# Layer 2's experts by tiles of slots, with weights addressed by registers, and first loads in another order

## The chip, the cores and the metric

The kernel runs on one core of one Trainium2 chip. The metric is the device time of one execution in microseconds (us), as a median of runs. All arithmetic is in float32.

## What is computed

Four decoder-like layers act one after the other on 4 sequences of 512 tokens with 256 features. Each normalises its input and adds an attention part and a feed-forward part to it:

```python
xn = _layernorm(x); x = x + mamba2(xn) + glu(xn)                  # layer 0
xn = _layernorm(x); x = x + latent_attention(xn) + product_key_experts(xn)   # layer 1
xn = _layernorm(x); x = x + head_mix(xn) + _L2_ffn_ref(xn, ...)   # layer 2
xn = _layernorm(x); x = x + full_attention(xn) + top_p_experts(xn)  # layer 3

def _L2_ffn_ref(x, gate_w, wg, wu, wd, sg, su, sd):   # E, K, I = 8, 2, 128
    scores = jax.nn.softmax(jnp.einsum('th,eh->te', xf, gate_w), axis=-1)
    topk_w, topk_i = jax.lax.top_k(scores, K)
    topk_w = topk_w / jnp.sum(topk_w, axis=-1, keepdims=True)
    cw = jnp.zeros_like(scores).at[jnp.arange(T)[:, None], topk_i].add(topk_w)
    g = jnp.einsum('th,ehi->eti', xf, wg)
    u = jnp.einsum('th,ehi->eti', xf, wu)
    eo = jnp.einsum('eti,eih->eth', jax.nn.silu(g) * u, wd)
    y = jnp.einsum('te,eth->th', cw, eo)
    shared = jax.nn.silu(xf @ sg) * (xf @ su) @ sd
    return y + shared
```

So in layer 2 every token has weights for two of eight experts of 128 hidden features each, and a shared expert of 256 hidden features besides. The reference computes all eight for every token; six of the eight weights are zero.

## The kernel before, in words

The residual `x` (16 tiles of 128 tokens by 256 features) and its normalised, transposed copy `xnT` (features on partitions) stay on the chip all the time. `layernorm(c, b)` does one sequence `b`: statistics and scaling on VectorE (lines 94 to 105), then, some pieces later, transposes on TensorE (line 114) that ScalarE copies into `xnT` (line 117). With an argument `tokens` it also writes the rows to a tensor in HBM (line 108), from which layer 1 reads.

Each layer is a set of Python generators that issue a piece of work and yield a number, its assumed cost. `weave` (line 205) always goes on with the generator whose share of its total is smallest, which fixes the program's order; a start of 0.95 lets a stream begin when the others stand at 95 per cent. The framework under it sets the waits and the buffers and may place an engine's instructions in another order than the program's where it estimates that one is ready earlier; `keep_in_program_order` holds one back from that. `c.parts(n, then)` says how many streams must report a sequence with `part_done` before `then` (a `layernorm`, or the store at the end) is issued for it.

Matrix products go through two helpers, `project` (line 125: weights stationary, tokens moving, 512 columns) and `project_tokens` (line 133). `glu_pieces` (line 156) computes a gated unit for one sequence after the other: for each 128 hidden features two products into PSUM, Silu on ScalarE (line 186), a product on VectorE (line 187), and then, for each tile of 128 tokens, the product down (line 194), which `add_scaled` adds to `x` (line 142, or line 144 with a factor per token).

Layer 2 (`layer2`, line 1174) has two streams. `ahead` does `head_mix` and `top2_weights` per sequence: the router's softmax and the rank of each expert by comparisons (`router`, line 1136) give `cw`, a weight per token and expert that is zero but for two. `expert_pieces` (line 1202) takes all eight experts as two units of 512 hidden features, four experts each; with `split=4` each expert's output is scaled by its column of `cw` on its way into `x`. Every token thus goes through all eight. The shared expert follows for each sequence.

Layer 1 has the latent attention (a stream of 457), the product-key experts (232), which gather rows of a table with indirect DMAs from GpSimd (line 917, 8 per tile of tokens), and a gated unit (193). Layer 3 has the full attention and, from 0.95 of it on, eight experts of 512 hidden features. At the start `program` loads `x` in four pieces on SyncE's queue and two tensors of constants on ScalarE's, then layer 0's first weights follow on SyncE's.

## Time and profile before

| | |
|---|---|
| median of 3 runs | 3283.12 us (3281.36 to 3287.85) |
| profiled execution | 3294.33 us, span of its instructions 3292.6 us |
| granted TensorE clock, mean | 0.989 |
| TensorE matmul (PE) busy | 3187.1 us, 97% |
| VectorE (DVE) busy | 1888.8 us, 57% |
| ScalarE (ACT) busy | 1259.1 us, 38% |
| GpSimd (POOL) busy | 565.3 us, 17% |
| DMA | 165.15 MB, mean 50 GB/s |

In the profile PE is TensorE's matmul, PEld its weight load, DVE is VectorE, ACT ScalarE, POOL GpSimd, SP SyncE. A line of a group of instructions gives line of the code, engine, operation, output and inputs, shapes and count, then after the bar the busy time in us and the mean of one in ns, and after the next bar the engine's idle time just before them and what ended it. A line of the order of time gives start and length in us (several alike are put together), and in brackets the idle time before it and its releaser. A "q" behind an engine's name means its sequencer. Matmuls are pipelined and their ends are modelled, so a busy PE is not PE at its peak. A duration comes from this one execution.

### The profile page before, as it was taken

The numbers are of one execution on the slowest core, as the hardware profiler recorded it, in microseconds if no ns is written. First come the engines' busy times: TensorE is split into PE (matmuls) and PEld (weight loads), VectorE is DVE, ScalarE is ACT, GpSimd is POOL, SyncE is SP. The second block draws the span as 40 slices with busy tenths as digits, with TensorE's granted clock in tenths as the row PEclk, the third lists the DMA queues.
The fourth block names the chain that finished last, engine by engine and source line by source line (L and its number), as shares of the span: only waits on it lengthen the run. The fifth ranks groups of instructions, "written<-read, shape, count | busy, mean of one in ns | idle before, by whom it ended". The sixth has DMA issues, their size and how long they took to land.

```text
span 3292.6 us, 35469 instructions
## 1 busy us (share of the span) xinstructions
PE 3187.1 (97%) x12524; PEld 1916.8 (58%) x12524; DVE 1888.8 (57%) x4720; ACT 1259.1 (38%) x2876; POOL 565.3 (17%) x445
## 2 busy tenths in 40 slices
PE   8999999998899999999999999999999999999999
PEld 4555656565555555555665556656656665555555
DVE  4777878887676776767665555455455522222222
ACT  4434444442455655657422333333333321111111
POOL 0455556546200122221010000000000000000000
PEclk9999999999999999999999999999999999999999
DMA  3232323323201343433000100000000010000000
GB/s 125 75 109 94 120 84 109 103 93 99 80 15 34 68 127 95 110 76 96 15 0 20 39 1 26 1 20 7 0 20 0 1 38 18 19 18 19 6 0 26
DMA packets 75650, 165.15 MB, mean 50 GB/s; under 512 B 12368, under 2 KB 46288, under 8 KB 70608
## 3 DMA queue, kind: packets, MB, share of 16 engines
q1 hardware_dynamic: 64368, 127.20, 12.0%
q0 software_dynamic: 10240, 33.56, 4.2%
q8 instruction: 99, 1.62, 0.2%
q10 hardware_dynamic: 864, 2.12, 0.2%
q14 instruction: 79, 0.65, 0.1%
HBM read 149.08 MB, written 4.85 MB: 47 GB/s over the span
## 4 chain that ended last, share of the span: by engine, by line
PE 76%; DVE 11%; DMA 4%; POOL 3%; ACT 3%; issue 2%; SPq 0%; another core or an unknown queue 0%; ACTq 0%; DVEq 0%; POOLq 0%
PE mm L125 31%; PE acc L194 10%; PE mm L577 8%; PE mm L133 4%; PE acc L1034 4%; PE acc L593 3%; DMA G<-own 3%; DVE cy L259 2%; DVE G L400 2%; PE tr L1026 2%; PE tr L756 2%; PE acc L800 2%; PE acc L813 2%; PE tr L486 1%; POOL y L449 1%
## 5 line engine op out<-in xcount | busy, mean ns | idle before, releaser
L125 PE MATMUL mm<-xnT,wu 128*128 128x512 f32 x2384 | 1074.6, 596 | 8.9 <-DVE cy L259 4.9
L125 PEld LDWEIGHTS mm<-xnT,wu 128*128 128x128 f32 x2384 | 450.4, 191 | 506.6 <-issue 472.0
L584 ACT ACTIVATE pr<-pr,nm 128x128 f32<-128x128 f32 (+3 forms) x512 | 286.0, 559 | 313.7 <-DVE nm L580 296.2
L186 ACT ACTIVATE sg<-mm 128x512 f32<-128x512 f32 x200 | 119.0, 595 | 681.6 <-PE mm L125 681.2
L187 DVE TENSOR_TENSOR hT<-sg,mm 128x512 f32<-128x512 f32 x200 | 137.0, 685 | 422.7 <-PE mm L125 408.1
L194 PE MATMUL acc<-wu,hT 128*128 128x256 f32 x1600 | 373.5, 381 | 0.0
L194 PEld LDWEIGHTS acc<-wu,hT 128*128 128x128 f32 x1600 | 299.6, 190 | 89.0 <-issue 34.8
L580 DVE CUSTOM_DVE_ANT_0 pr<-mm,late 128x128 f32<-128x128 f32 (+3 forms) x512 | 245.4, 483 | 99.8 <-PE mm L577 91.6
L125 PE MATMUL mm<-xnT,w_in 128*128 128x512 f32 x512 | 232.7, 599 | 6.1 <-DVE cy L259 4.5
L144 DVE SCALAR_TENSOR_TENSOR x<-acc,cw,x 128x256 f32<-128x256 f32 x256 | 123.4, 483 | 181.1 <-PE acc L194 175.8
L917 POOL DMA_INDIRECT e<-in_p_experts,ids x128 | 127.6, 997 | 506.3 <-DVE x L144 474.6
L400 DVE TENSOR_TENSOR_SCAN G<-G,eye 128x1024 f32<-128x1024 f32 x64 | 159.5, 2492 | 57.2 <-DMA G<-own 57.0
L577 PE MATMUL mm<-kf,qf 128*128 128x128 f32 (+3 forms) x512 | 176.4, 444 | 9.0 <-DVE qf L735 6.0
L577 PE MATMUL mm<-k,q 128*128 128x128 f32 (+3 forms) x512 | 178.5, 438 | 1.1 <-issue 0.9
L426 POOL TENSOR_TENSOR G<-G,CB 128x1024 f32<-128x1024 f32 x64 | 151.1, 2361 | 158.7 <-ACT CB L352 81.0
L259 DVE SCALAR_TENSOR_TENSOR cy<-mm,ws,cy 128x509 f32<-128x509 f32 (+2 forms) x216 | 158.6, 741 | 29.3 <-ACT cy L255 26.0
L125 PEld LDWEIGHTS mm<-xnT,w_in 128*128 128x128 f32 x512 | 97.4, 192 | 111.1 <-issue 98.4
L412 ACT ACTIVATE xD<-xc,ws 128x128 f32<-128x128 f32 x256 | 84.3, 391 | 200.3 <-POOL y L449 194.4
L142 DVE TENSOR_TENSOR x<-acc,x 128x256 f32<-128x256 f32 x176 | 74.0, 422 | 139.8 <-PE acc L593 102.5
L1034 PE MATMUL acc<-PT,V 128*128 128x512 f32 (+3 forms) x512 | 150.2, 436 | 0.0
L999 DVE TENSOR_SCALAR q<-mm,bias 128x512 f32<-128x512 f32 x64 | 48.1, 751 | 169.9 <-PE mm L125 169.9
L486 PE MATMUL tr<-wo,y 128*128 128x256 f32 x512 | 130.1, 398 | 9.4 <-DVE x L142 3.8
(246 smaller groups left out, 4649.7 us busy)
## 6 DMA issues: line engine op xcount, KB each, us to landing
G<-own SPq DMA_DIRECT2D x64, 512.0 KB
w_in<-in_m_units SPq DMA_DIRECT2D x16, 1024.0 KB
eb<-since SPq DMA_DIRECT2D x96, 128.0 KB
wu<-in_o_units SPq DMA_DIRECT2D x8, 1536.0 KB
wo<-in_m_units SPq DMA_DIRECT2D x16, 512.0 KB
psw<-pes SPq DMA_DIRECT2D x128, 64.0 KB
wu<-in_g_units SPq DMA_DIRECT2D x4, 1536.0 KB
wu<-in_f_units SPq DMA_DIRECT2D x4, 1536.0 KB
```

The lines of the kernel that those rows point to most:

```text
L125: c.nc.tensor.matmul(out, lhsT=w[:, d, cols], rhs=c.xnT[:, d, tokens], start=(d == 0), stop=(d == 1))
L133: c.nc.tensor.matmul(out, lhsT=c.xnT[:, d, tokens], rhs=w[:, d, cols], start=(d == 0), stop=(d == 1))
L187: nc.vector.tensor_mul(h, sg, pu)
L194: nc.tensor.matmul(po, lhsT=hT[k][:, t * P : (t + 1) * P], rhs=wd[:, k, :], start=(i == 0), stop=(i == per - 1),)
L259: nc.vector.scalar_tensor_tensor(y[:, j:], src[:, : SEQ - j], conv[:, k, 3 - j : 4 - j], y[:, j:], ALU.mult, ALU.add,)
L400: nc.vector.tensor_tensor_scan(flat, flat, eye.rearrange("p h t -> p (h t)"), 0.0, ALU.mult, ALU.add)
L426: nc.gpsimd.tensor_mul(G, G, seqs[b][2][:, t, :][:, None, :].to_broadcast([P, HG, P]))
L486: nc.tensor.matmul(po, lhsT=y[:, k, :], rhs=groups[i][1][:, k, :], start=(k == 0), stop=(k == 3))
L577: nc.tensor.matmul(sc, lhsT=q[:, i * P : n], rhs=k[:, :n], start=True, stop=True)
L580: nc.vector.tensor_tensor_reduce(out=pr, in0=sc, in1=late[:, SEQ - n :], scale=1.0, scalar=-NEG, op0=ALU.add, op1=ALU.min, accum_out=nm,)
L584: nc.scalar.activation(pr, pr, AF.Exp, bias=nm, scale=-1.0, accum_out=total)
L1034: nc.tensor.matmul(z[:, j * P :], lhsT=head["V"][:, j, h, :], rhs=head["PT"][:, j, j * P :], start=(j == 0), stop=(j == TPB - 1),)
```

## The change

Layer 2's tokens are treated in two halves of 1024 (`Half`). `dispatch` ranks the experts as before and then, for each token and each of its two experts, computes a slot: tokens of one expert get consecutive slots, and each expert's slots are filled up to a multiple of 128, at most 23 tiles of slots per half. It yields `ids` (which token stands in a slot), `slot` (where a token's two results will be), `weight`, and `expert` (where the weights of each tile's expert begin). `experts` goes through the 23 tiles in pairs: an indirect DMA gathers the normalised rows of a tile's tokens, TensorE turns them, and one expert's matrices, taken out of a tile with all weights at a column held in a register of TensorE, are applied; the results are written to HBM by slots. `combine` gathers each token's two rows and adds them with their weights to `x`.

The order changes with it. The first half's `dispatch` is a fourth stream of layer 1 from 0.915 on, after the buffers of two other streams were closed; layer 1's `layernorm` writes its rows to HBM for the gathers. `Layer2.run` issues the second half's `dispatch`, then weaves the first half's experts with `head_mix` and the shared expert, then the second half's experts with the first half's `combine`. The second half's `combine` is a stream of layer 3. The buffers of several stages change sides in SBUF. Layer 3 adds its output bias per sequence in the third group of heads instead of at its start. At the kernel's start `first_loads` issues all first loads on SyncE's queue: `x` in five pieces, between them the identity alone, the first unit's gate and up weights in two parts, and the rest of the constants and the down weights last; `layernorm` of the input moves into `layer0`.

```diff
@@ layernorm
-            r = b * SEQ + t * P
-            nc.sync.dma_start(tokens[r : r + P, :], xn)
+            nc.sync.dma_start(tokens[t * P : (t + 1) * P, :], xn)
@@ layer0
+def first_loads(c, a, x_in, con, ws, unit):
+    nc = c.nc
+    load = nc.sync.dma_start
+    def tokens(lo, hi):
+        load(
+            c.x[:, lo:hi, :], x_in[lo * P : hi * P, :].rearrange("(t p) d -> p t d", p=P)
+        )
+    def chunks(k):
+        part = lambda v: v[:, :2048].rearrange("p (m j) -> p m j", j=512)[:, :, k * P : (k + 2) * P]
+        load(part(unit), part(a["g0_units"][0]))
+    tokens(0, 2)
+    tokens(2, 4)
+    load(con[:, :P], a["constants"][:, :P])
+    chunks(0)
+    tokens(4, 8)
+    load(ws, a["m_small"])
+    tokens(8, 12)
+    tokens(12, 16)
+    chunks(2)
+    load(con[:, P:], a["constants"][:, P:])
+    load(unit[:, 2048:], a["g0_units"][0][:, 2048:])
+def layer0(c, a, x_in, con):
...
+        unit = c.tile(c.weights, [P, 3072], "wu")
+        ws = c.tile(open_pool("m_ws", 1), [P, 762], "ws")
+        first_loads(c, a, x_in, con, ws, unit)
+        for b in range(NB):
+            layernorm(c, b)
+            c.step(True)
...
+        def glu_units():
+            same = dict(bufs=5, out_tag="tr")
+            yield from glu_pieces(c, glu, [unit], loaded=True, last=False, **same)
+            yield from glu_pieces(c, glu, [a["g0_units"][1]], first=1, **same)
+        c.parts(2, lambda b: layernorm(c, b, c.xn[b * SEQ : (b + 1) * SEQ, :]))
...
@@ layer1
+def layer1(c, a, xn, following):
+    with ExitStack() as stack, ExitStack() as right:
+        def pool_of(name, bufs, stack=stack, **kw):
+            return stack.enter_context(c.tc.tile_pool(name=name, bufs=bufs, **kw))
+        p_keep, p_t, glu = (pool_of(name, 1, right, side="right") for name in ("p_keep", "p_t", "g1"))
+        dram = pool_of("p_dram", 1, space=bass.MemoryType.DRAM)
+        keep = pool_of("l_keep", 1)
         prep = c.tc.tile_pool(name="l_pre", bufs=2)
         latent = latent_pieces(c, a, keep, prep, lambda: pool_of("l_h", 2))
+        def route():
+            right.close()
+            yield from following.route()
         weave(
             c,
             (latent, 457.0, 0.0),
             (product_key_pieces(c, a, p_keep, p_t, dram, xn), 232.0, 0.0),
             (glu_pieces(c, glu, [a["g1_units"][u] for u in range(2)], tanh=True, bufs=5), 193.0, 0.0),
+            (route(), 150.0, 0.915),
         )
...
@@ full_attention
-        for t in range(NTILE):
-            nc.gpsimd.tensor_add(c.x[:, t, :], c.x[:, t, :], bias[:, 48:])
...
+                    if g == 2:
+                        nc.gpsimd.tensor_add(c.x[:, tt, :], c.x[:, tt, :], bias[:, 48:])
@@ layer 2
-def top2_weights(c, pool, wr, cw, b):
...
-def layer2(c, a):
...
-def expert_pieces(c, pool, a, by_token):
...
+E8, HT, NS = 8, NTILE // 2, 23
+EW = 6 * P
+class Half:
+    def __init__(self, c, k, pool, keep, dram, hf, xn):
+        self.c, self.k, self.pool, self.hf, self.xn = c, k, pool, hf, xn
+        self.out = c.tile(dram, [NS * P, DM], "slots_out")
+        new = lambda shape, tag, dtype=F32: c.tile(keep, shape, tag, dtype, bufs=2)
+        self.ids = new([P, NS], "ids", U32)
+        self.slot = new([P, 2 * HT], "slot", U32)
+        self.weight = new([P, 2, HT], "weight")
+        self.expert = new([P, NS], "expert", I32)
+    def dispatch(self):
+        c, k, pool, nc = self.c, self.k, self.pool, self.c.nc
+        tile = lambda shape, tag, **kw: c.tile(pool, shape, tag, **kw)
+        p, rank = tile([P, HT, E8], "p_half"), tile([P, HT, E8], "rank")
+        for i in range(2):
+            tiles = slice(i * TPB, (i + 1) * TPB)
+            before = router(c, pool, k["router"], 2 * self.hf + i, p[:, tiles, :])[2]
+            nc.vector.tensor_reduce(rank[:, tiles, :], before, AX.X, ALU.add)
+            yield 1.0
+        both = [P, 2, HT, E8]
+        sel = tile(both, "sel")
+        for r in range(2):
+            nc.vector.tensor_scalar(sel[:, r], rank, float(r), None, ALU.is_equal)
+        chosen = tile([P, HT, E8], "chosen")
+        nc.vector.tensor_scalar(chosen, rank, 2.0, None, ALU.is_lt)
...
+        pc = c.ps()
+        n = HT * E8
+        nc.tensor.matmul(pc[:, :n], lhsT=c.le, rhs=flat(chosen), start=True, stop=False)
+        nc.tensor.matmul(pc[:, :n], lhsT=c.ones, rhs=flat(cum[:, :HT, :]), start=False, stop=True)
+        nc.tensor.matmul(
+            pc[:, n : n + E8], lhsT=c.ones, rhs=cum[:, HT, :], start=True, stop=True
+        )
+        yield 1.0
...
+        nc.vector.tensor_mul(pick, sel, place[:, None, :, :].to_broadcast(both))
+        nc.vector.tensor_reduce(
+            slot, pick.rearrange("p r t e -> p (r t) e"), AX.X, ALU.add
+        )
+        nc.vector.tensor_copy(self.slot, slot)
+        yield 1.0
...
+        pid = c.ps()[:, :NS]
+        for i in range(2 * HT):
+            at = tile([P, P], "at", bufs=3)
+            t = i % HT
+            nc.vector.tensor_scalar(
+                at, k["iota"], part[:, i : i + 1], k["token"][:, t : t + 1],
+                ALU.is_equal, ALU.mult,
+            )
+            nc.tensor.matmul(
+                pid, lhsT=at, rhs=hit[:, i, :], start=(i == 0), stop=(i == 2 * HT - 1)
+            )
+            if i % 4 == 3:
+                yield 1.0
+        nc.vector.tensor_copy(self.ids, pid)
...
+        nc.vector.tensor_copy(self.expert[:1], where[:1])
+        yield 1.0
...
+    def experts(self, weights, xpool, pool, opool):
+        c, nc = self.c, self.c.nc
+        pairs = [[t for t in (2 * j, 2 * j + 1) if t < NS] for j in range((NS + 1) // 2)]
+        xs, xsT, hs, hT = {}, {}, {}, {}
+        def gather(j):
+            xs[j] = c.tile(xpool, [P, 2, DM], "xs", bufs=3)
+            for i, t in enumerate(pairs[j]):
+                nc.gpsimd.indirect_dma_start(
+                    out=xs[j][:, i, :], out_offset=None, in_=self.xn,
+                    in_offset=bass.IndirectOffsetOnAxis(ap=self.ids[:, t : t + 1], axis=0),
+                )
+        def turn(j):
+            pt = c.ps("tr")
+            n = len(pairs[j])
+            for i in range(n):
+                for d in range(2):
+                    nc.tensor.transpose(
+                        pt[:, (2 * i + d) * P : (2 * i + d + 1) * P],
+                        xs[j][:, i, d * P : (d + 1) * P], c.ident,
+                    )
+            xsT[j] = c.tile(pool, [P, 4, P], "xsT", bufs=2)
+            nc.scalar.copy(xsT[j][:, : 2 * n, :], v3(pt[:, : 2 * n * P], P))
+        def hidden(j):
+            ph = v3(c.ps(), 2 * P)
+            n = len(pairs[j])
+            for i, t in enumerate(pairs[j]):
+                for d in range(2):
+                    nc.tensor.matmul(
+                        ph[:, i, :], lhsT=xsT[j][:, 2 * i + d, :],
+                        rhs=weights[:, bass.ds(where[t] + 2 * d * P, 2 * P)],
+                        start=(d == 0), stop=(d == 1),
+                    )
+            sg = c.tile(pool, [P, 2, P], "gate", bufs=2)
+            hs[j] = c.tile(pool, [P, 2, P], "hs", bufs=2)
+            nc.scalar.activation(sg[:, :n, :], ph[:, :n, :P], AF.Silu)
+            nc.vector.tensor_mul(hs[j][:, :n, :], sg[:, :n, :], ph[:, :n, P:])
+        def turn_hidden(j):
+            pt = c.ps("tr")
+            n = len(pairs[j])
+            for i in range(n):
+                nc.tensor.transpose(pt[:, i * P : (i + 1) * P], hs[j][:, i, :], c.ident)
+            hT[j] = c.tile(pool, [P, 2, P], "hsT", bufs=2)
+            nc.scalar.copy(hT[j][:, :n, :], v3(pt[:, : n * P], P))
+        def down(j):
+            po = v3(c.ps("acc"), DM)
+            n = len(pairs[j])
+            for i, t in enumerate(pairs[j]):
+                nc.tensor.matmul(
+                    po[:, i, :], lhsT=hT[j][:, i, :],
+                    rhs=weights[:, bass.ds(where[t] + 4 * P, DM)], start=True, stop=True,
+                )
+            os = c.tile(opool, [P, 2, DM], "os", bufs=2)
+            nc.vector.tensor_copy(os[:, :n, :], po[:, :n, :])
+            rows = self.out[2 * j * P : (2 * j + n) * P, :]
+            nc.sync.dma_start(rows.rearrange("(i p) d -> p i d", p=P), os[:, :n, :])
+        where = []
+        N = len(pairs)
+        gather(0)
+        gather(1)
+        for lo in (0, 12):
+            where.extend(nc.values_load_multi_w_load_instructions(
+                self.expert[:1, lo : min(lo + 12, NS)], engines=[mybir.EngineType.PE],
+                min_val=0, max_val=(E8 - 1) * EW,
...
+            )[1])
+        turn(0)
+        yield 0.5
+        for j in range(N + 2):
+            if j + 2 < N:
+                gather(j + 2)
+            if j < N:
+                hidden(j)
+                yield 1.7
+            if j >= 2:
+                down(j - 2)
+                yield 0.9
+            if j + 1 < N:
+                turn(j + 1)
+            if 1 <= j <= N:
+                turn_hidden(j - 1)
+            yield 0.6
+    def combine(self, pool):
+        c, nc = self.c, self.c.nc
+        for t in range(HT):
+            tt = self.hf * HT + t
+            for r in range(2):
+                row = c.tile(pool, [P, DM], "row", bufs=4)
+                nc.gpsimd.indirect_dma_start(
+                    out=row, out_offset=None, in_=self.out,
+                    in_offset=bass.IndirectOffsetOnAxis(
+                        ap=self.slot[:, r * HT + t : r * HT + t + 1], axis=0
+                    ),
+                )
+                add_scaled(c, tt, row, self.weight[:, r, t : t + 1])
+            if tt % TPB == TPB - 1:
+                c.part_done(tt // TPB)
+            yield 1.0
+class Layer2:
...
+    def route(self):
+        c, a = self.c, self.a
+        keep, route, self.xs = self.pool("t_keep"), self.pool("t_route"), self.pool("t_xs")
+        dram = self.pool("t_dram", space=bass.MemoryType.DRAM, side="left")
+        small = c.tile(keep, [P, 152], "t_small")
+        c.nc.gpsimd.dma_start(small, a["t_small"])
+        self.weights = c.tile(keep, [P, E8 * EW], "weights")
+        c.nc.gpsimd.dma_start(self.weights, a["t_experts"])
+        k = dict(router=v3(small[:, :16], 8), iota=small[:, 16:144], token=small[:, 144:])
+        self.halves = [Half(c, k, route, keep, dram, hf, self.xns[hf]) for hf in range(2)]
+        yield from self.halves[0].dispatch()
+    def run(self):
+        c, a = self.c, self.a
+        for _ in self.halves[1].dispatch():
+            pass
+        self.rows = self.pool("t_rows")
+        with ExitStack() as stack:
+            temp, mixer = self.pool("t_temp", stack), self.pool("h_t", stack)
+            h_small = c.tile(mixer, [P, 864], "h_small")
+            c.nc.sync.dma_start(h_small, a["h_unit"])
+            unit = c.unit(a["t_shared"])
+            def mix():
+                for b in range(NB):
+                    yield from head_mix(c, mixer, h_small, b)
+            shared = glu_pieces(c, mixer, [unit], n=2, width=256, loaded=True, bufs=4)
+            experts = [
+                half.experts(self.weights, self.xs, temp, self.rows) for half in self.halves
+            ]
+            weave(c, (experts[0], 38.0, 0.0), (mix(), 12.0, 0.0), (shared, 41.0, 0.0))
+            weave(c, (experts[1], 38.0, 0.0), (self.halves[0].combine(self.rows), 12.0, 0.0))
+    def rest(self):
+        yield from self.halves[1].combine(self.rows)
+        self.stack.close()
@@ layer3
-def layer3(c, a):
-    weave(c, (full_attention(c, a), 765.0, 0.0), (top_p_experts(c, a), 765.0, 0.95))
+def layer3(c, a, ahead, store):
+    def attention():
+        yield from full_attention(c, a)
+    def rest():
+        yield from ahead
+        c.parts(2, store)
+    weave(
+        c, (rest(), 110.0, 0.0), (attention(), 765.0, 0.0), (top_p_experts(c, a), 765.0, 0.95)
+    )
@@ program
-        xn = c.tile(dram, [NT, DM], "xn_tokens")
-        for b in range(NB):
-            layernorm(c, b)
-            c.step(True)
-        c.parts(2, lambda b: layernorm(c, b, xn))
-        layer0(c, a)
+        c.xn = c.tile(dram, [NT, DM], "xn_tokens")
+        layer0(c, a, x_in, con)
         c.weights = stack.enter_context(tc.tile_pool(name="weights", bufs=3))
+        halves = [c.tile(dram, [NT // 2, DM], "xn_half") for _ in range(2)]
+        c.parts(3, lambda b: layernorm(c, b, halves[b // 2][b % 2 * SEQ : (b % 2 + 1) * SEQ, :]))
+        second = Layer2(c, a, halves)
+        layer1(c, a, c.xn, second)
         c.parts(3, lambda b: layernorm(c, b))
-        layer1(c, a, xn)
-        c.parts(1, lambda b: layernorm(c, b))
-        layer2(c, a)
+        second.run()
-        c.parts(2, store)
-        layer3(c, a)
+        layer3(c, a, second.rest(), store)
```

## The prediction, on record before the result

> **What bounds the kernel now.** I read the page first (parts 1 and 4), then the busy time by stretches of layer 2, then its groups of instructions, the order of time, and the rows nearest to the new operations.
>
> ```profile
> PE 3187.1 (97%) x12524; PEld 1916.8 (58%) x12524; DVE 1888.8 (57%) x4720; ACT 1259.1 (38%) x2876; POOL 565.3 (17%) x445
> PE 76%; DVE 11%; DMA 4%; POOL 3%; ACT 3%; issue 2%; SPq 0%; another core or an unknown queue 0%; ACTq 0%; DVEq 0%; POOLq 0%
> ...
> 1560.00:1590.00 30.00, 28.36 (x157) 19.13 (x156) 20.14 (x66) 22.73 (x60) 0.00 (x0) 1.00 0.10 32
> 1590.00:1650.00 60.00, 58.92 (x210) 35.13 (x209) 41.22 (x105) 17.09 (x26) 3.85 (x2) 1.00 0.06 21
> 1750.00:1810.00 60.00, 60.00 (x199) 35.39 (x198) 32.42 (x78) 13.40 (x19) 2.98 (x4) 1.00 0.07 27
> ```
>
> The last three lines are stretches (length, then PE, PEld, DVE, ACT, POOL busy, clock, DMA share, GB/s). PE is full through layer 2 (about 1600 to 1824 us) and nothing else is near full. A busy PE may still be slow, so I check its spacing in the order of time:
>
> ```profile
> 1655.27 1.89 PE L194 MATMUL acc<-wu,hT 128*128 128x256 f32 x8
> 1660.44 4.88 PE L125 MATMUL mm<-xnT,wu 128*128 128x512 f32 x11
> ...
> 32.70 1.04 PE L114 MATMUL tr<-con,xn 128*128 128x128 f32 x8
> ```
>
> A single pass lasts longer than the distance to the next, since passes overlap. Distances: (1.89 - 0.38)/7 = 0.215 us for 256 columns, (4.88 - 0.59)/10 = 0.43 us for 512, (1.04 - 0.28)/7 = 0.108 us for 128. The groups of 1590 to 1825 us say how many passes there are:
>
> ```profile
> L144 DVE SCALAR_TENSOR_TENSOR x<-acc,cw,x 128x256 f32<-128x256 f32 x128 | 61.5, 483 | 28.7 <-PE acc L194 23.4 <-DVE x L144 0.5
> L125 PE MATMUL mm<-xnT,wu 128*128 128x512 f32 x320 | 148.4, 592 | 0.0
> L187 DVE TENSOR_TENSOR hT<-sg,mm 128x512 f32<-128x512 f32 x40 | 27.4, 686 | 49.6 <-PE mm L125 47.1 <-ACT sg L186 2.3
> ```
>
> 40 hidden tiles need 160 calls of line 125 and show 320 records: each call is two passes. So layer 2 costs PE, for its eight experts on all tokens, 32 tiles x 8 passes x 0.43 = 110.1 us, and 128 calls of line 194 x 2 x 0.215 = 55.0 us: **165.1 us**; the shared expert is 8 x 8 x 0.43 + 32 x 2 x 0.215 = 41.3 us. With head_mix (32 calls of 288 columns, 0.242 us a pass, 15.5 us) that fills the 224 us. PE work taken out here is time, as long as no new wait replaces it.
>
> **The change, part by part.** *PE work of the experts.* The new tiles are fixed in number (23 a half, padded), so the work does not depend on the data. A tile: two transposes in, 4 x 0.108; two calls of 256 columns, 4 x 0.215; one transpose, 2 x 0.108; one call down, 2 x 0.215: 1.94 us. 46 tiles are 89.1 us. Routing adds to each half 16 calls on `at` (2 x 0.108 each) and three small ones: 4.1 us, 8.2 for both; the router's own calls stay. Balance: -165.1 + 89.1 + 8.2 = **-67.8 us**.
>
> *Other engines of that loop.* DVE loses 128 x 0.483 and 32 x 0.686 (83.8 us) and gets, per pair of tiles, a product (0.42, as 256 columns at L142) and a copy (0.69 at most): 26.6 us, 32 scaled adds 15.5 us, and routing beyond the router some 12 us a half (50 small operations, most like 0.16 to 0.42 us rows). ACT gets per pair three rows of at most 0.60 us: 1.8 us against 3.87 us of PE. Neither binds: nothing.
>
> *Gathers.* A POOL gather in layer 1 (order of time, then the tensor's view; last, two rows for the next step, by line):
>
> ```profile
> 1113.58 0.95 POOL L917 DMA_INDIRECT e<-in_p_experts,ids  x1 [0.30 <-DVE nm L580]
> 1117.83 1.15 POOL L917 DMA_INDIRECT e<-in_p_experts,ids  x1 [0.30 <-issue]
> ...
> DMA to landing us min/median/max: 4.5/5.4/8.7
> ...
> L584 ACT ACTIVATION_READ_ACCUMULATOR pr<-pr,nm x512: 184/187/198, 908.0 to 2652.0; 128x1 f32 x171
> ...
> L577 PEldq EVENT_SEMAPHORE  x56: 51/51/6328, 906.8 to 2639.2; - x56
> ```
>
> One costs POOL 0.95 + 0.30 = 1.25 us, at most 1.42 + 0.30. The first half's 23 (29 us) lie beside experts, head_mix and shared expert (44.5 + 15.5 + 41.3 us of PE). The second half is alone: 12 pairs, 44.5 us of PE, and POOL has 23 gathers plus the first half's 16 of `combine`: 39 x 1.25 = 49 us, up to 67. Behind a `combine` gather that waits for a free `row` (4 buffers) or for the first half's rows to land, the next tiles' gathers wait too, POOL being in order, and PE waits for them. Also `turn(j+1)` is followed by only 0.43 us of transposes before `hidden(j+1)` needs ACT's 0.59 us copy. The two overlap. Ends 0 (work of layer 3 fills the holes) and +22; I take **+7**, nearest to 49 against 44.5 with a little for the copies. Bytes: 8 MB in 45 us is 178 GB/s, and the first loads ran above 400: nothing.
>
> *Registers on PE.* No row shows one. 46 values are read on PE's queue, which stands meanwhile with all matmuls behind it. The nearest rows that read one value out are ACT's accumulator read, 0.187 us, and DVE's, 0.084: 3.9 to 8.7 us; hidden, 0. I take **+6**. The 138 calls with a register in their address need some one or two sequencer steps each; at PE's semaphore step, 0.051 us, that is 7 to 14 us if all are in the open, 0 if the sequencer runs ahead, which 0.43 us of passes per call favours. I take **+3**. [...]
>
> *Routing of the first half, in layer 1's tail.* About 19 us of DVE (6.8 of it the routers that were there before) enter a stretch where DVE is busy 20.14 of 30 us and ACT 22.73 and where PE waits for both in the attention. The 16 extra row writes go through SP, 0.3 to 0.55 us each, beside that attention's swaps. Ends 0 (free thirds of DVE hold it) and +12 (all new DVE work on the path); **+4**. The second half's routing has 100 us of PE work beside it: nothing; without that cover, its chain, some 25 us. The 3.1 MB of weights come on POOL's queue, idle there, well before use: nothing.
>
> *The hand-over to layer 3.* Before, the first sequence was normalised long before its use; now it needs `combine`, and the second half's `combine` runs beside layer 3, whose first two sequences offer some 96 us of PE work. Ends 0 and +10, a landing of 5.4 and the layernorm's chain; **+4**. The POOL bias adds (16 x 0.765 us) move to a time when POOL is idle: nothing.
>
> *First loads.* DMA is saturated for the first 22 us, and PE waits, then crawls:
>
> ```profile
> 9.72 2.19 PE L114 MATMUL tr<-con,xn 128*128 128x128 f32 x8 [9.72 <-DVE xn L102]
> ...
> 19.02 3.46 PE L133 MATMUL mm<-ws,xnT 128*128 128x32 f32 x16
> ...
> 29.79 1.28 PE L133 MATMUL mm<-ws,xnT 128*128 128x32 f32 x10
> ```
>
> A pass takes 0.21 us at 19 us and 0.11 at 30: half speed until about 28 us. Smaller first pieces let PE start perhaps 2 us earlier and have glu work sooner, but later on PE waits for the mamba preparation (52 to 64 us), which can eat it. Ends -8 (half of the 18 us idle before 28 us) and 0; **-3**. [...]
>
> **Sum.** -67.8 + 7 + 6 + 3 + 4 + 4 - 3 = -46.8. The profiled execution took 3294.3 us (span 3292.6), 11 us above the median of the runs; from 3283.1 it gives **3236 us**. All ends at their best: -76, 3207. All at their worst: -67.8 + 22 + 8.7 + 14 + 12 + 10 = -1, 3282.
>
> **The rivals.** *All saving lands* (chance 0.12): holes are filled with layer 3's work and the start wins; 3207 to 3215. For it: PE's order here mixes work of neighbouring stages (layer 1's transposes stand among head_mix's matmuls at 1584 us). Against it: the loop has six hand-overs per pair.
>
> *Half is lost* (0.21): the first half's routing ends late. It gets only the free third of DVE, so its 25 us chain takes 60 or more; head_mix and the shared expert are spent as cover before the experts start, and then 24 pairs, not 12, run alone. At 1.3 us lost a pair that is 31 instead of 7: -23, **3260 to 3285**.
>
> *Slower than before* (0.12): the loop is paced by its gathers. Gather, landing and the steps of a pair are 2 x 1.25 + 5.4 + 0.7 + 0.6 + 1.9 + 0.6 + 0.7 + 0.6 + 0.6 + 1.0 + 0.7, about 15 us if nothing overlaps, against 3.87 us of PE; three `xs` buffers should hide the first 8. If POOL's queue stands behind `combine` or the buffers, the period rises. The first half has 56.8 us, 4.7 a pair, of other work; so only the second pays until 8.6 us. Without the +7, the sum is -54, and 12 x (period - 3.87) makes that up at 8.4 us: there it decides. At 10 us the price is 74 + 17 = 91: -54 + 91 = +37, **3320 us**.
>
> The forecast itself keeps 0.55, as PE's balance is counted row by row and the cover is there for half of the loop; its own range is 3215 to 3260.
>
> **How the numbers follow.** Faster by over 0.2% (6.6 us, about what a measurement of this kernel can tell from no change): forecast, full saving and most of the half-lost case, 0.83. Within 0.2%: its end, 0.05. Slower: 0.12. The range 3207 to 3290 takes in the bounds of the unknown costs and the half-lost case, and leaves out the slower rival.
>
> **What would show it.** Right: of layer 2's 320 passes of line 125 only the 64 of the shared expert are left, PE near 97% still, a layer 2 of about 175 us instead of 224, gathers 1.25 us apart in the second half, holes of PE under 1 us a pair there. Registers: gaps of 2 to 5 us on PE twice a half mean the loads. Wrong: pairs more than 6 us apart in the second half, PE idle long at 1530 to 1610 us, or idle at layer 3's start behind `combine`. A change of more than 10 us outside layer 2 and the first 60 us would mean that I missed a part of the change.

## The result, and the profile after

The changed kernel took 3290.84 us (median of 16 runs), the kernel before 3284.07 us beside it. The ratio is 1.0021, 95% interval 1.0012 to 1.0031: 7 us slower, where I had forecast 47 us faster. The profiled execution took 3299.62 us, with a span of 3297.8 us; it is 9 us above its median, and the one before (3294.33 us) is 10 above its own.

The page's busy time, and its chain of waits:

```profile
PE 3142.2 (95%) x12502; PEld 1916.6 (58%) x12502; DVE 1859.9 (56%) x4730; ACT 1263.1 (38%) x2911; POOL 650.2 (20%) x525
PE 74%; DVE 11%; DMA 5%; POOL 4%; ACT 3%; issue 3%; SPq 0%; another core or an unknown queue 0%; DVEq 0%; ACTq 0%; POOLq 0%
```

PE is busy 45 us less than before, and yet the span is 5 us longer. The groups of PE between 1590 and 1825 us say that the work went as counted: line 125 has 64 passes left of 320, and the tiles' 92 calls with an address from a register (184 passes) are there.

```profile
L1371 PE MATMUL mm<-weights,xsT 128*128 x184 | 48.1, 405 | 7.6 <-ACT xsT L1364 6.7 <-ACT s L1159 0.6 <-issue 0.3
L125 PE MATMUL mm<-xnT,wu 128*128 128x512 f32 x64 | 34.6, 674 | 0.0
```

The same stretches as before (length, then PE, PEld, DVE, ACT, POOL busy, clock, DMA share, GB/s) show where it was given back. PE had 28.36, 58.92 and 60.00 us in them at a clock of 1.00:

```profile
1560.00:1590.00 30.00, 25.92 (x107) 19.65 (x104) 19.45 (x75) 14.10 (x34) 0.00 (x0) 0.69 0.20 71
1590.00:1650.00 60.00, 44.75 (x180) 30.77 (x180) 28.48 (x108) 17.87 (x38) 11.43 (x12) 0.64 0.17 46
1750.00:1810.00 60.00, 36.25 (x166) 29.27 (x165) 25.73 (x65) 16.59 (x34) 34.24 (x34) 0.80 0.47 130
```

There are three holes, each at a low clock. The first is layer 1's tail. The second, in order of time, is the start of layer 2:

```profile
1627.89 0.69 PE L1253 MATMUL mm<-chosen,con 128*128 128x64 f32 x2 [4.62 <-DVE chosen L1245]
...
1635.63 1.48 PE L1309 MATMUL mm<-hit,at 128*128 128x23 f32 x6 [5.30 <-DVE at L1305]
...
1649.51 2.05 PE L125 MATMUL mm<-xnT,wu 128*128 128x512 f32 x2
1651.36 2.92 PE L1371 MATMUL mm<-weights,xsT 128*128 x8
```

PE waits for the second half's routing, with `head_mix` and the shared expert behind it in its queue; two passes of 512 columns then take 2.05 us instead of some 1.02 (0.43 and a pass of 0.59), half speed. The first expert tile comes 38.6 us after layer 1's last product (1612.8 us). The third hole lies between the halves:

```profile
1764.94 1.99 PE L1371 MATMUL mm<-weights,xsT 128*128 x8 [0.51 <-ACT xsT L1364]
1768.91 1.99 PE L1371 MATMUL mm<-weights,xsT 128*128 x8 [0.46 <-ACT xsT L1364]
...
1791.96 1.94 PE L114 MATMUL tr<-con,xn 128*128 128x128 f32 x8 [16.17 <-DVE x L144]
...
1798.30 3.78 PE L1371 MATMUL mm<-weights,xsT 128*128 x8 [2.40 <-ACT xsT L1364]
```

The loop itself is as counted: a pair every 3.97 us against 3.87 us of work. But the transposes of the first sequence's `layernorm` stand in PE's queue ahead of the next tiles and wait 16.17 us for `combine`'s additions. Those wait for rows, and GpSimd fetches rows 1.25 us apart without a break from 1769 to 1794 us, 20 in all, the tiles' gathers (line 1349) among those of `combine` (line 1436):

```profile
1774.42 0.95 POOL L1349 DMA_INDIRECT xs<-xn_half,ids  x1 [0.30 <-issue]
1775.67 0.97 POOL L1349 DMA_INDIRECT xs<-xn_half,ids  x1 [0.30 <-issue]
1776.94 0.94 POOL L1436 DMA_INDIRECT row<-slots_out,slot  x1 [0.30 <-DVE hs L1379]
1778.19 0.94 POOL L1436 DMA_INDIRECT row<-slots_out,slot  x1 [0.30 <-issue]
```

In windows of 4 us from 1500 to 1900 us, PE is idle 63.7 us (before: 9.6), and its busy time times the missing part of the clock is 36.4 us (before: 3.3).

### The profile page after: what moved, and what is told of

Read it like the earlier page. It is cut to its first block, busy times and chain, and to the rows that moved or that the text cites. A ratio compares the mean times of both kernels' runs of the same rounds, so it can differ in the third digit from the quotient of the medians.

```text
span 3297.8 us, 35820 instructions
## 1 busy us (share of the span) xinstructions
PE 3142.2 (95%) x12502; PEld 1916.6 (58%) x12502; DVE 1859.9 (56%) x4730; ACT 1263.1 (38%) x2911; POOL 650.2 (20%) x525
## 4 chain that ended last, share of the span: by engine, by line
PE 74%; DVE 11%; DMA 5%; POOL 4%; ACT 3%; issue 3%; SPq 0%; another core or an unknown queue 0%; DVEq 0%; ACTq 0%; POOLq 0%
PE mm L125 28%; PE acc L194 9%; PE mm L616 8%; PE mm L133 5%; PE acc L1078 4%; PE acc L632 3%; DMA G<-own 2%; DVE cy L257 2%; PE tr L1070 2%; PE tr L795 2%; DVE G L398 2%; PE acc L839 2%; PE acc L852 2%; PE tr L484 1%; POOL y L447 1%
## 5 line engine op out<-in xcount | busy, mean ns | idle before, releaser
L125 PE MATMUL mm<-xnT,wu 128*128 128x512 f32 x2128 | 956.8, 597 | 7.0 <-DVE cy L257 2.6
L125 PEld LDWEIGHTS mm<-xnT,wu 128*128 128x128 f32 x2128 | 401.6, 191 | 465.1 <-issue 436.3
L187 DVE TENSOR_TENSOR hT<-sg,mm 128x512 f32<-128x512 f32 x168 | 115.2, 686 | 385.6 <-PE mm L125 373.3
L186 ACT ACTIVATE sg<-mm 128x512 f32<-128x512 f32 x168 | 99.9, 595 | 598.1 <-PE mm L125 597.9
L194 PE MATMUL acc<-wu,hT 128*128 128x256 f32 x1344 | 307.0, 382 | 6.7 <-DVE x L142 6.3
L194 PEld LDWEIGHTS acc<-wu,hT 128*128 128x128 f32 x1344 | 253.0, 191 | 60.7 <-issue 19.5
L125 PEld LDWEIGHTS mm<-xnT,w_in 128*128 128x128 f32 x512 | 96.6, 191 | 109.5 <-issue 97.7
L144 DVE SCALAR_TENSOR_TENSOR x<-acc,cw,x 128x256 f32<-128x256 f32 x128 | 61.9, 484 | 152.4 <-PE acc L194 152.4
L795 PE MATMUL tr<-con,pr 128*128 128x128 f32 x640 | 127.6, 289 | 15.8 <-ACT pr L788 7.5
L795 PEld LDWEIGHTS tr<-con,pr 128*128 128x128 f32 x640 | 82.0, 146 | 103.5 <-ACT pr L788 37.4
```

The source lines that it names most:

```text
L125: c.nc.tensor.matmul(out, lhsT=w[:, d, cols], rhs=c.xnT[:, d, tokens], start=(d == 0), stop=(d == 1))
L194: nc.tensor.matmul(po, lhsT=hT[k][:, t * P : (t + 1) * P], rhs=wd[:, k, :], start=(i == 0), stop=(i == per - 1),)
L795: nc.tensor.transpose(pt[:, (i - j) * P : (i - j + 1) * P], prs[s][i][:, j * P : (j + 1) * P], c.ident)
```

## The experiments

My theory after the result: the work saved did come off PE and was paid back as waits *around* the expert tiles, at those three places, with the low clock on top. The rivals: the tiles are slow themselves (gathers, registers); the first loads cost something.

The table has, for each kernel, its ratio to the kernel before on the same chip, the *tail* (from score 448 to layer 1's last product; scores are the 512 records of layer 1's products of queries and keys, counted from 0) and *layer 2* (from there to layer 3's first score), both from the order of time of one profiled execution, in us. *Combine later*, *tail halved* and *routing filled* were measured together at another time, when the kernel before took 3269.9 us instead of some 3290, so only ratios are compared across them.

| kernel | ratio (95%) | tail | layer 2 |
|---|---|---|---|
| before | 1 | 84.8 | 239.5 |
| changed | 1.0021 (1.0012 to 1.0031) | 103.6 | 227.5 |
| first loads alone | 0.9999 (0.9988 to 1.0011) | 84.6 | 239.2 |
| both dispatches in one piece | 1.0024 (1.0012 to 1.0036) | 87.8 | 244.3 |
| second routing woven | 0.9948 (0.9928 to 0.9968) | 96.9 | 206.5 |
| transposes later | 1.0036 (1.0023 to 1.0049) | 97.7 | 229.2 |
| constant columns | 1.0003 (0.9990 to 1.0017) | 97.0 | 224.2 |
| hole between halves filled | 1.0024 (1.0010 to 1.0038) | 103.8 | 227.8 |
| one row gather | 0.9977 (0.9966 to 0.9987) | 98.0 | 216.4 |
| cover for gathers | 0.9898 (0.9883 to 0.9914) | 96.3 | 195.0 |
| tail free | 0.9964 (0.9949 to 0.9979) | 83.5 | 233.4 |
| combine later | **0.9873** (0.9854 to 0.9892) | 96.4 | 179.9 |
| tail halved | 0.9931 (0.9916 to 0.9945) | 88.7 | 214.2 |
| routing filled | 0.9992 (0.9981 to 1.0004) | 100.2 | 221.6 |

Two parts of the kernel stand in neither column. Up to score 448 the changed kernel is 5.8 us ahead (1509.2 us against 1515.0), and from layer 3's first score to the end it takes 1457.6 us against 1453.2. By stage the 5 us of the span are thus -5.8 + 18.8 - 12.0 + 4.4. Each entry comes from one execution, and the tails of kernels with the same code there lie between 96.3 and 103.8 us, so a difference of a few us between two rows says nothing.

**First loads alone.**

```diff
@@ the kernel before: first_loads, layer0, mamba_pieces and program as in the change
+        first_loads(c, a, x_in, con, ws, unit)
```

> The kernel before with the new order of the first loads alone, and nothing of the new layer 2. My theory (the work saved in layer 2 came, and was given back as new waits of PE around the expert tiles, not inside them, each of them made dearer by a clock that falls to half): the start itself wins 6 to 10 us, as the profile after has the first scores of layer 1 9.2 us earlier than before; ratio 0.9970 to 0.9982. My prediction's term was 3 us: 0.9991. Rival A (the first loads are what costs the time, a gain at the start being lost again in layer 0): ratio 1.000 or above.

0.9999: nothing, within 4 us. PE starts at 7.1 us instead of 9.7, and layer 1's first scores come at 898.5 us instead of 906.9; but score 256 has a lead of 3.4 us left (1246.6 against 1250.0) and score 448 is 1.0 us late (1516.0). My theory's 6 to 10 us are wrong, and so, in this execution, is rival A's loss in layer 0: the lead lasts through layer 0 and is lost inside layer 1. Which of layer 1's waits takes it was not settled; between 1100 and 1200 us PE is busy 94.78 us there and 99.35 before. Nor is it shown that it is always lost there: in the nine kernels of the table that have the new layer 2 and ran beside a kernel before of 3284 to 3291 us, score 448 comes between 1499.0 and 1514.7 us, all ahead of the 1515.0 before.

**The second routing woven in.**

```diff
@@ Layer2.run
-        for _ in self.halves[1].dispatch():
-            pass
...
-            weave(c, (experts[0], 38.0, 0.0), (mix(), 12.0, 0.0), (shared, 41.0, 0.0))
+            weave(
+                c, (mix(), 12.0, 0.0), (shared, 41.0, 0.0), (experts[0], 38.0, 0.0),
+                (self.halves[1].dispatch(), 16.0, 0.0),
+            )
```

> The changed kernel, but the second half's dispatch is not issued in one piece ahead of everything in layer 2: it is a fourth stream beside head_mix, the shared expert and the first half's expert tiles. My theory: the hole of PE at 1613 to 1650 us, in which PE waits for VectorE's routing steps at half clock while head_mix and the shared expert stand behind them, closes; 15 to 25 us less than the changed kernel, so about 3266 to 3276 us, ratio to the kernel before 0.994 to 0.998. Rival B (gathers and register addresses slow the expert tiles, the holes around them only show time that would be lost anyway): under 5 us, ratio 1.000 to 1.003.

0.9948 against 1.0021: 24 us less (within 7). Layer 2 takes 206.5 us instead of 227.5, and the first tile comes 15 us after layer 1's end (1601.4 us), at full speed:

```profile
1616.56 1.97 PE L1371 MATMUL mm<-weights,xsT 128*128 x8 [0.28 <-issue]
```

Rival B falls: the tiles are the same.

**The transposes later.**

```diff
@@ layernorm; in Layer2.run c.delay is 40 during the second weave
-    c.later.append([8, turn])
+    c.later.append([c.delay, turn])
```

> The changed kernel, but the transposes of a layernorm that the first half's combine triggers are issued 40 pieces later instead of 8, so behind the second half's expert tiles in PE's queue. My theory: the wait of 16 us at 1775 us goes and the clock stays up behind it; some of it comes back at layer 3's start, where the first transposes are then needed: 8 to 18 us less than the changed kernel, 3273 to 3283 us, ratio 0.997 to 1.000. Rival C (the wait only moves: VectorE and GpSimd are late in any case, and layer 3 starts no earlier): 0 to 4 us, ratio 1.001 to 1.003, and the idle time stands at layer 3's start instead.

No gain (1.0036): the wait only moved, as rival C has it, though not to layer 3's start alone. PE's waits from 1740 to 1850 us:

```profile
PE mm L1372 <- ACT xsT L1365: 22.1, 8, 15.2
PE mm L617 <- issue: 7.0, 1, 7.0
```

The next tile (line 1372 in this kernel) now waits 15.2 us for its turned rows. In order of time on ScalarE, which copies them:

```profile
1767.04 0.30 ACT L84 ACTIVATE rsq<-mv,eps 128x4 f32<-128x4 f32 x1 [3.92 <-DVE x L145]
1774.21 0.58 ACT L1365 COPY xsT<-tr 128x512 f32<-128x512 f32 x1 [6.87 <-remote]
```

The copy stands behind the `layernorm`'s square root, and that behind VectorE's additions of the gathered rows. (After it the copy waits 6.87 us more for something that the trace does not name; that stays open.) So PE's queue is only the first of several in which the tiles' work stands behind `combine`'s rows; to reorder this one alone gained nothing.

**One row gather.**

```diff
@@ Half.combine
             for r in range(2):
+                if r:
+                    add_scaled(c, tt, row, self.weight[:, r, t : t + 1])
+                    continue
                 row = c.tile(pool, [P, DM], "row", bufs=4)
```

> The changed kernel with 8 gathers in each combine instead of 16: it leaves out the second result of each token and adds the first one with both weights. Theory 1 (GpSimd's queue paces the hand-over): the wait at 1775 us falls from 16 to 10 us or less, as about half of the gathers that stand ahead of the first sequence's rows and of the next tiles go; 5 to 12 us less than the changed kernel, ratio 0.9985 to 1.0005. Theory 2 (latency through HBM and VectorE's chain): the wait stays at 13 to 16 us, ratio 1.001 to 1.003.

0.9977, 14 us less than the changed kernel (within 5), and the wait at the transposes is halved. PE's waits from 1760 to 1850 us:

```profile
PE tr L114 <- issue: 7.6, 1, 7.6
PE mm L616 <- issue: 4.2, 1, 4.2
```

Eight gathers less at 1.25 us are 10 us, and the wait is 8.6 us shorter: the number of gathers sets it, not a fixed latency. Theory 2 falls.

**Cover for the gathers** (on top of the routing woven in).

```diff
@@ Layer2.run
-                c, (mix(), 12.0, 0.0), (shared, 41.0, 0.0), (experts[0], 38.0, 0.0),
+                c, (mix(), 12.0, 0.0), (experts[0], 38.0, 0.0),
...
-            weave(c, (experts[1], 38.0, 0.0), (self.halves[0].combine(self.rows), 12.0, 0.0))
+            weave(
+                c, (shared, 41.0, 0.0), (experts[1], 38.0, 0.0),
+                (self.halves[0].combine(self.rows), 12.0, 0.0),
+            )
```

> The run with the second half's dispatch woven in, and one thing more: the shared expert (41 us of PE) stands beside the second half's tiles instead of the first half's. Theory 1 (GpSimd's queue paces the hand-over between the halves: 16 gathers of combine and the next tiles' gathers, 1.25 us each, go through it one after the other, and PE has nothing else to do): the 16 us of waiting there shrink to under 5, and the time falls by 10 to 18 us more, to about 3250 to 3258 us, ratio to the kernel before 0.989 to 0.992. Theory 2 (the wait is the latency of the results' way through HBM, the transposes of the first sequence are needed then in any case): the wait moves to layer 3's start, under 4 us of gain, ratio 0.994 to 0.996.

0.9898, 16 us less than with the routing woven in alone (within 9), as theory 1 has it: the same work in the stretch where GpSimd is the slower engine. The one wait of 16 us has become these, from 1680 to 1850 us:

```profile
PE acc L194 <- DVE x L144: 7.8, 1, 7.8
PE mm L616 <- DVE q L1043: 5.4, 2, 5.2
PE acc L194 <- DVE os L1398: 3.8, 1, 3.8
```

**Combine later** (on top of that).

```diff
-                (self.halves[0].combine(self.rows), 12.0, 0.0),
+                (self.halves[0].combine(self.rows), 12.0, 0.25),
```

> The run with the shared expert beside the second half's tiles, and combine of the first half starting a quarter of a half later. Theory: the wait of 7.8 us that was left there (shared expert's sums behind combine's additions in VectorE's queue, which wait for their rows) shrinks under 3 us; 4 to 8 us less, ratio to the kernel before 0.987 to 0.989. Rival (combine's end then comes too late for layer 3's first products): gain 0 or a loss up to 5 us, idle time of PE at layer 3's start over 8 us instead of 5.

0.9873, 41 us less than the kernel before: the version that beats both. The wait of 7.8 us at line 194 is gone; the longest one inside the loop is now 3.0 us. The step itself, 0.25% against the run before it, is as large as its uncertainty. Windows of this kernel:

```profile
1590.00:1650.00 60.00, 53.86 (x293) 45.56 (x294) 42.18 (x122) 25.63 (x44) 24.14 (x21) 0.97 0.30 78
1650.00:1710.00 60.00, 55.37 (x234) 40.25 (x233) 35.22 (x78) 19.98 (x39) 37.64 (x36) 0.97 0.38 113
```

The clock is back at 0.97. From 1500 to 1900 us PE is idle 30.0 us and the clock's loss is 12.8 us.

**The tail: dispatch out of it, in three ways.** Wholly, in one piece at layer 2's start:

```diff
@@ Layer2.route and run
-        yield from self.halves[0].dispatch()
+        yield 0.0
...
-        for _ in self.halves[1].dispatch():
-            pass
+        for half in self.halves:
+            for _ in half.dispatch():
+                pass
```

> The changed kernel with one edit: the first half's dispatch leaves layer 1's tail and is issued in one piece at layer 2's start, ahead of the second half's, which stays as it is. Theory (the dispatch in the tail costs 12 to 19 us there, and a dispatch without cover costs its chain of about 25 us): score 448 to layer 1's last product takes 83 to 86 us instead of 97 to 104; from there to the first product of layer 3's scores 20 to 35 us more than the 228 of the changed kernel; net 3 to 20 us slower than the changed kernel, ratio to the kernel before 1.003 to 1.008. Rival (the tail is long for another reason, such as the layernorm's writes to HBM or the closed buffers): the tail stays above 95 us, ratio 1.006 to 1.012.

The tail falls to 87.8 us, layer 2 rises by 17 us (I expected 20 to 35), and the ratio (1.0024) is that of the changed kernel, a little under the 1.003 that I had as the least. So the tail's 12 to 19 us are the dispatch, and are paid again where it goes; the rival falls.

Wholly, beside other work (`shared` and `shared2` are the shared expert's two halves):

```diff
@@ Layer2.route
-        yield from self.halves[0].dispatch()
+        yield 0.0
@@ Layer2.run
...
+            weave(c, (mix(), 12.0, 0.0), (shared, 20.0, 0.0), (self.halves[0].dispatch(), 12.0, 0.0))
+            weave(c, (experts[0], 38.0, 0.0), (self.halves[1].dispatch(), 16.0, 0.0))
+            weave(
+                c, (shared2, 20.0, 0.0), (experts[1], 38.0, 0.0),
+                (self.halves[0].combine(self.rows), 12.0, 0.0),
+            )
```

> The first half's dispatch is taken out of layer 1's tail and put beside head_mix and half of the shared expert; then come the first half's tiles with the second half's dispatch, then the second half's tiles with combine and the other half of the shared expert. Theory 1 (the dispatch in the tail delays layer 1's last heads by 12 us or more, since its VectorE work stands in front of theirs): layer 1's last product comes 85 us after score 448 as in the kernel before (103 in the changed one), and the time falls to 3240 to 3252 us, ratio 0.986 to 0.990. Rival (the tail is bound by ScalarE and the chain of the last heads anyway; the dispatch has to stand somewhere): the same as with the dispatch in the tail, 3252 to 3262 us.

And from the one-hot products on (on top of *combine later*):

```diff
-        yield from self.halves[0].dispatch()
+        self.first = self.halves[0].dispatch()
+        for _ in range(5):
+            yield next(self.first)
@@ Layer2.run
-            weave(
-                c, (mix(), 12.0, 0.0), (experts[0], 38.0, 0.0),
-                (self.halves[1].dispatch(), 16.0, 0.0),
-            )
+            weave(c, (self.first, 6.0, 0.0), (mix(), 12.0, 0.0))
+            weave(c, (experts[0], 38.0, 0.0), (self.halves[1].dispatch(), 16.0, 0.0))
```

> The run before this one, with the first half's dispatch cut in two: up to the slots it stays in layer 1's tail, the 16 one-hot products and what follows stand beside head_mix at layer 2's start. Theory 1 (about half of the VectorE work of the dispatch leaves the tail): the tail from score 448 to layer 1's last product takes 88 to 92 us instead of 96 to 103, the first expert tile comes about 12 us later after layer 1's end than now, covered by head_mix; net 0 to 5 us of gain, ratio 0.986 to 0.989. Theory 2 (as in the run with the whole dispatch out of the tail, what is won there is paid twice in layer 2): a loss of 5 to 15 us against the run before this one.

Both shorten the tail as expected (83.5 and 88.7 us) and lose more in layer 2: the first is 22 us slower than the kernel with all cover beside the gathers, the second 19 us slower than *combine later*. In the first, PE waits 10.5 us for `chosen` and 10.1 us at the change of halves; in the second, 11.6 us for `head_mix`'s additions. My expectation of a gain was wrong: none of the three versions is cheaper than the tail. Only the first of the three moves the dispatch alone; the other two also take cover away elsewhere (half of the shared expert from the gathers, `head_mix` from the first half's tiles), so what their place for the dispatch costs by itself is not shown.

**Constant columns.**

```diff
-                        rhs=weights[:, bass.ds(where[t] + 2 * d * P, 2 * P)],
+                        rhs=weights[:, where[t] + 2 * d * P : where[t] + 2 * d * P + 2 * P],
...
@@ Half.experts, in place of the loads into registers
+        where.extend(t * E8 // NS * EW for t in range(NS))
```

> The changed kernel, but the columns of the weights are constants instead of values in registers: it leaves out the choice of the expert by the data (tile t takes the matrices of expert 8t/23), and no register is loaded or added up on TensorE. My theory: the register loads (4.9 us in four places, partly hidden) and the sums (6 us on the sequencer, mostly hidden) are worth 0 to 6 us; ratio to the kernel before 1.000 to 1.002. Rival B (register addressing slows the loop): 15 us or more, ratio 0.997 to 0.998 or below.

1.0003: 6 us less than the changed kernel, within 6. Registers are a small term, and rival B falls again. In the changed kernel, by line (duration min/median/max in ns):

```profile
L1407 PEldq TENSOR_LOAD <-expert x4: 857/1183/1723, 1648.1 to 1794.8; - x4
...
L1371 PEldq FUSED_REGOPS  x92: 42/44/51, 1649.3 to 1821.4; - x92
```

**Useless products in the holes.** First in the hole between the halves:

```diff
@@ layernorm.turn, first sequence only
+            pf = c.ps()
+            for _ in range(16):
+                c.tc.keep_in_program_order(
+                    nc.tensor.matmul(pf, lhsT=c.ident, rhs=c.con, start=True, stop=True)
+                )
```

> The changed kernel with 16 products of 512 columns by the identity, whose result nobody reads (14 us of PE), ahead of the first sequence's transposes that PE waits for at 1775 us. Nothing is taken away. Theory (a hole of some us costs a second time, because the clock falls to half and stays there for a while after PE has work again): the 8 transposes take 1.04 us instead of 1.94, the tile behind them 1.9 instead of 3.8, the granted clock stays near 1.0 at 1780 to 1800 us, and the time falls by 2 to 7 us against the changed kernel; ratio 0.999 to 1.0015. Rival (the slow passes have another cause): passes as slow as before, and the time rises by up to 2 us.

```profile
1769.10 13.90 PE L118 MATMUL mm<-con 128*128 128x512 f32 x32
1785.98 1.68 PE L123 MATMUL tr<-con,xn 128*128 128x128 f32 x8 [2.98 <-DVE x L153]
...
1792.86 1.12 PE L1368 MATMUL tr<-con,xs 128*128 128x128 f32 x4 [3.25 <-ACT xnT L126]
...
1794.87 3.37 PE L1380 MATMUL mm<-weights,xsT 128*128 x8 [0.46 <-ACT hsT L1396]
```

The clock held through the filled 14 us (1.00 from 1768 to 1784 us), then fell in the smaller waits of 2.98 and 3.25 us behind them (0.50 from 1788 to 1796 us), and the next tile was slow again (3.37 us instead of 1.99). No gain (1.0024): the tile behind the stretch starts 27.6 us after the tile ahead of it, against 25.4 in the changed kernel. That the gathers set the pace there is argued from the two runs above with fewer gathers and with cover, not shown by this one. Then in the second half's routing:

```diff
@@ Half.dispatch, second half only: 6 behind the router, 7 ahead of the one-hot products
+            pf = c.ps()
+            for _ in range(6):
+                c.tc.keep_in_program_order(
+                    nc.tensor.matmul(pf, lhsT=c.ident, rhs=c.con, start=True, stop=True)
+                )
...
```

> The changed kernel with 13 products of 512 columns by the identity, read by nobody, put into the second half's dispatch: 6 behind its router, 7 ahead of its one-hot products. Nothing is taken away; it fills two of the waits in the hole at 1613 to 1650 us. Theory (the low clock is a price of its own: after the waits PE runs the products of 1636 to 1652 us at half speed): the granted clock there is 0.9 or above, those 16 us take about 9, and the time falls by 2 to 7 us, ratio to the kernel before 0.9995 to 1.0015. Rival (the stretch is paced by VectorE's 16 one-hot steps and their turns with PE, whatever the clock): the same or up to 5 us longer, ratio 1.002 to 1.0035.

0.9992: 13 products that nobody reads make the kernel 9.5 us faster than the changed one (within 5). In order of time, beside the lines of 1635 to 1651 us above:

```profile
1605.33 0.74 PE L1321 MATMUL mm<-hit,at 128*128 128x23 f32 x6
...
1611.92 1.10 PE L125 MATMUL mm<-xnT,wu 128*128 128x512 f32 x2
1612.86 0.52 PE L1321 MATMUL mm<-hit,at 128*128 128x23 f32 x4
1614.52 1.99 PE L1383 MATMUL mm<-weights,xsT 128*128 x8 [1.14 <-issue]
```

The same stretch takes 9.2 us instead of 15.7 (1605.33 to 1614.52, 1635.63 to 1651.36), with 1.10 us for two passes instead of 2.05. Here the clock was a price of its own.

## Why the prediction was wrong, point by point

Forecast -46.8 us, measured +7: 54 us to account for.

- **PE's work** (-67.8): right in kind. The passes that were to go are gone, and a pair takes 3.97 us against 3.87. PE's busy time fell by 45 us and not by 68, as passes at half clock are busy twice as long (2.05 us instead of some 1.02 for two of 512 columns): between 1500 and 1900 us the low clock takes 33 us more of it than before (36.4 against 3.3). Of the signs that I had named, the 64 passes and the gathers 1.25 us apart came; layer 2 was to fall by 49 us and fell by 12.
- **Routing of the second half** ("100 us of PE work beside it: nothing; without that cover, its chain, some 25 us"): the step that failed. The price without cover was near (24 us, within 7), partly by luck, as 9.5 of the 24 us (within 5) are the low clock, which I had not priced; the choice was wrong. The work was beside it in the list of things to do, not in PE's queue: `run` issues the whole dispatch first, and what follows in program order was mostly behind it. Its 24 us came back when it was woven in. I had the order in front of me and did not ask what stands behind the waiting product.
- **Gathers of the second half** (+7, ends 0 and 22): mechanism right, size too small. GpSimd's 39 gathers against 44.5 us of PE looked like a close race over the whole half; but 20 gathers, the tiles' and `combine`'s, came in one block near its start, and PE, ScalarE and VectorE each had the tiles' work queued behind something that waits for their rows. Cover is worth 16 us there, and leaving out 8 gathers in each `combine` 14.
- **Routing of the first half in the tail** (+4, ends 0 and 12): 12 to 19 us by the tails of 96.3 to 103.8 us against 84.8, beyond my worse end. From 1500 to 1600 us PE is busy 89.66 us against 92.28 before, but at a clock of 0.86 instead of 0.97, so more of this is slow passes than idle time. I priced VectorE's work and not the clock. The stretch before, then after:

```profile
1500.00:1600.00 100.00, 92.28 (x432) 54.89 (x431) 72.53 (x232) 71.72 (x183) 10.07 (x9) 0.97 0.17 50
1500.00:1600.00 100.00, 89.66 (x405) 56.83 (x403) 69.17 (x259) 63.40 (x161) 12.07 (x13) 0.86 0.33 95
```

- **First loads** (-3, ends -8 and 0): nothing within 4 us. The early start was seen, and in that run lost in layer 1; why stays open.
- **Registers** (+6 and +3): 6 us within 6 by the run with constants. The four loads took 4.9 us together, 0.11 us a value, inside the bounds of 0.084 and 0.187 that I had from the accumulator reads (46 of the latter are 8.6 us, not 8.7); the 138 sums are 0.042 to 0.051 us each on the sequencer and mostly hidden (6.2 us in all, in 6.1 of which PE has products running).
- **Hand-over to layer 3** (+4, ends 0 and 10): inside the ends, but nearer 8 than 4. Ahead of layer 3's first scores PE waits 4.9 us, for `q`, instead of 0.9, and the eight passes behind the wait take 4.52 us instead of 2.40. From there to the end the changed kernel takes 4.4 us more than the one before; these passes are 2 of them, the rest was not followed, nor what holds `q` back. Before, then after:

```profile
1839.33 2.40 PE L577 MATMUL mm<-k,q 128*128 128x128 f32 x8 [0.89 <-issue]
1840.29 4.52 PE L616 MATMUL mm<-k,q 128*128 128x128 f32 x8 [4.94 <-DVE q L1043]
```

- **Not in the sum at all**: in the first half PE waited 8.2 us in four places for VectorE's additions to `x` (lines 194 and 1393 behind line 142). The likely reason, argued from this line and not tried: `head_mix`'s last addition waits 3.5 us each time for a product on GpSimd, and the shared expert's additions stand behind it on VectorE.

```profile
L1167 DVE TENSOR_TENSOR x<-x,prod 128x1024 f32<-128x1024 f32 x4 | 4.9, 1225 | 14.1 <-POOL prod L1162 14.1
```

Together: 24 for the second routing, 9 more for the gathers, some 11 more for the tail, 3 for the first loads, 8 for those waits, some 4 more for the hand-over, about -3 for the registers: 56 us, where 54 are to be accounted for. That they come so near is partly luck: the differences between runs are known within 5 to 9 us, the other sizes are read from single executions, and the terms are not independent, as the clock is in several of them.

Of the rivals, *half is lost* named the first half's routing as the late one; the second's did it. *Slower* named gathers behind `combine` on GpSimd, which happened once, at the change of halves, and not in every pair. With that one hole counted in, the second half's pairs are 6.3 us apart on average (from 1752.02 to 1821.42 us), over the 6 us that I had named as a sign of being wrong and under this rival's 8.4. The best version's 41 us are close to the forecast of 47: the saving was there for a schedule that has the cover I took for granted.

## What to carry to other kernels

Ask of a chain what work stands *ahead* of its waiting instruction in the same queue; here 100 us of work issued behind it hid little. When a change adds DMAs to one engine's queue, compare them with the other engines' work in each stretch, not over the whole, and put the free work where that queue is the slower one. Price a hole of several us in a TensorE-bound stretch at its length plus what the passes behind it lose at half clock (here 9.5 us of 24, within 5); filling the other hole won nothing.

## What the runs showed of the hardware that I had not expected

- The clock. In the second routing the granted clock was 0.50 from 1620 to 1650 us, though PE ran products without a pause from 1635.6 us on; its passes took twice their time (2.05 us for two of 512 columns) until about 1653 us. Filling the waits with unread products of 512 columns removed that: the first stands at 1590.16 us, and the clock is 0.75 on average from 1590 to 1600 us and 1.00 from there to 1630. Which passes bring the clock up, and why these took so much less time, was not tried by itself. After the 16.17 us hole the passes were back at full speed some 12 us later (two transposes take 0.63 us at 1795.27 us and 0.38 at 1804.05), with a wait of 2.40 us among them.
- How long PE works at the kernel's start before its passes are fast varies. In the changed kernel PE works from 10.64 us on and its passes are at full speed from 16.3 us at the latest (14 passes from 14.61 us on already take 1.86 us, where the other kernel's take 3.03); with the first loads alone it works from 10.62 us on, with the same instructions, and they are slow until about 27 us:

```profile
22.56 2.06 PE L125 MATMUL mm<-xnT,wu 128*128 128x512 f32 x2
...
27.62 1.10 PE L125 MATMUL mm<-xnT,wu 128*128 128x512 f32 x2
```

That the clock is the reason is inferred from the factor of two alone: the profile's clock column reads 1.00 from 0 to 32 us in both kernels, through the slow passes too. From the start of that work to the first fast passes it is 4 to 6 us in one kernel (10.64 to 14.61 or 16.30 us) and 17 us in the other (10.62 to 27.62 us), and the second routing has some 17 us of products at half clock (1635.6 to 1653 us). No run shows a reason for the difference.

- A load of 11 or 12 values into registers of TensorE took 0.86 to 1.72 us, and a sum for an address 0.042 to 0.051 us.
